# Block 2's context attention: a new first pass, its logits and norms moved among the feed-forward's products, and the weights' loads placed in the first pass

## The chip, the cores and the metric

The kernel runs on one core of one Trainium2 chip. A time is the device time of one execution in microseconds (us). The profile names the engines PE (TensorE matmuls; PEld is its weight loads), DVE (VectorE), ACT (ScalarE), POOL (GpSimd) and SP (SyncE, which here only issues DMAs). Its times are counted from the start of the span of one profiled execution.

## The reference

Four transformer blocks of the same width run one after the other over x, 4 sequences of 1024 tokens with 288 columns; the context has 64 tokens of 288 columns per sequence. Block 2 (`_L2_xattn_ref`) is the one that matters: self attention, then attention to the context, then a gated feed-forward, each added to x. Its second half is:

```python
n2 = _ln(h, ln2_g, ln2_b)
h = h + _quant_attention(n2, ctx, Wq2, Wk2, Wv2, Wo2, bo2)
n3 = _ln(h, ln3_g, ln3_b)
a, gate = jnp.split(n3 @ Wff1 + bff1, 2, axis=-1)      # 288 -> 2 x 1152
h = h + a * jax.nn.gelu(gate, approximate=False) @ Wff2 + bff2

# in _quant_attention, 16 heads of 18 columns:
q, k, v = _fake_quant(q, 8), _fake_quant(k, 8), _fake_quant(v, 8)
probs = softmax(q k^T / sqrt(18))
probs = _fake_quant(probs, 8, always_zero=True)        # delta = max over ALL probs / 255
out = (probs v) @ Wo + bo
```

The step of the probabilities' quantization is the maximum over every token, head and sequence. So all logits must be seen once (largest probability and sum of each row) before the first probability can be rounded, and the context attention takes two passes.

## The kernel before, in words

x stays on the chip as 32 tiles of 128 tokens (`self.x`). `fq_tail` does the second half of block 2. It receives the queries' raw values in DRAM (`rawq`) and the keys and values in three block-diagonal forms (`kbd4`, `kbd`, `vbd`), also in DRAM.

First pass, one tile of 128 tokens at a time: the queries are rounded to levels on DVE (L818, L819, L3426), transposed on PE (L3432), copied by ACT to `qT` (L3436) and stored to `qb` in DRAM (L3437). Four matmuls give the logits of 16 heads by 64 keys with the tokens on the partitions (L3442); ACT takes the exponential (L3449), DVE the largest of each head (L3455), POOL adds halves and quarters (L3457, L3459), and DVE sums what is left (L3460). After the 32nd tile `prob_shift` works out the step and a shift for each row of logits (L2546 to L2560, L836 to L844).

Then the loads for the feed-forward are issued: `w1` (3456 KB, L2582), `w2` (1296 KB, L114), the bias (L3476) and three broadcasts by POOL (L108).

Second pass, in groups of four tiles (512 tokens). `probs(t0)` loads `qT` back (L3486), adds the shift (L2567 on POOL, L2573 on PE, L2574 on DVE), takes the logits with the keys on the partitions (L3500, L3504), rounds them (L3506), multiplies by the values (L3512, L3519) and by `wo` (L278), and adds to x (L3525). `forward(t0)` takes the norm's statistics (L1437 to L1468), norms each tile (ACT L1485, POOL L1488 and L1489, with the bias added to x by POOL at L1877), transposes it (`width_T`: L2591, L2596, copy L2603), does the first product in blocks of four columns of 128 (`product4`: L2611, L2615), the gated Gelu (L3552, L3556), and the second product (L3564) that is added to x (L3572). A float32 matmul of the source is two instructions in the trace. The two are interleaved by `weave`: `probs` of one group with `forward` of the group before it and eight pieces of `spare`, which prepares block 3's weights (L1629 to L1700).

The order in which the source calls is not the order on the engines: a scheduler places the instructions by priority, engine by engine, and allocates the tiles from pools with a fixed number of buffers; each engine then executes in its order. Every DMA of these stages but the POOL broadcasts is issued by SP, in one queue. In the second pass two PSUM pools are in use, `pf` with five buffers for the first product and `pb` (`ps1`) with three for everything else. The normed tile `h` has two buffers.

Of the kernel before, what the change touches and what calls it, by code (L numbers as in the profile page):

```python
# [28 lines left out]
F32 = mybir.dt.float32  # L29
BF16 = mybir.dt.bfloat16  # L30
I32 = mybir.dt.int32
AF = mybir.ActivationFunctionType
ALU = mybir.AluOpType
AX = mybir.AxisListType
PSUM = bass.MemoryType.PSUM

P = 128
B, S, C, H, D, T, FF = 4, 1024, 288, 16, 18, 64, 1152
NTB = S // P
# [1140 lines left out]
class Fast(Net):  # L1180
# [2204 lines left out]
    def fq_tail(self, w, kq, keep, rawq, mx, nmn, beside):  # L3385
# [5 lines left out]
        with ExitStack() as es:  # L3391
# [3 lines left out]
            nc.sync.dma_start(wo, w["Wo2p"].rearrange("(g p) o -> p g o", p=P))  # L3395
            kt = {k: gp.tile(keep[k][1], BF16, name=k) for k in ("kbd", "vbd")}
            qb = [dr.tile([P, NG, S], BF16, name=f"qb{b}") for b in range(B)]
            with (
                self.psum8("f2"),
                tc.tile_pool(name="f2q", bufs=1) as qp,  # L3400
                self.work("f2k0", 3),
            ):
                kt["kbd4"] = qp.tile(keep["kbd4"][1], BF16, name="kbd4")
                for k, (d, _) in keep.items():
                    nc.sync.dma_start(kt[k], d)
                top = qp.tile([P, NT, H], F32, name="top")
                sums = qp.tile([P, NT, H], F32, name="sums")
                qn = qp.tile([P, NT, C], F32, name="qn")
                for b in range(B):
                    nc.sync.dma_start(qn[:, b * NTB : (b + 1) * NTB, :], rawq[b])  # L3410
                pads = [qp.tile([P, H, HP], BF16, name=f"pads{n}") for n in range(3)]
                for pd in pads:
                    nc.gpsimd.memset(pd, 0.0)
                q = self.global_params(gp, mx, nmn, "qq")
                self.watch_range(-0.5, 255.5, q["zp"], "qzext")
                step = gp.tile([P, 1], F32, name="step")
                nc.vector.tensor_scalar(
                    step, q["d"], kq["d"][:, 0:1], SCALE, ALU.mult, ALU.mult
                )
                rstep = self.scale_register("cstep", step)  # L3420

                for t in range(NT):
                    b, j = divmod(t, NTB)
                    pd = pads[t % 3]
                    self.fq_levels(qn[:, t, :], q, 0)
                    nc.vector.tensor_scalar(  # L3426
                        pd[:, :, :D], self.heads(qn[:, t, :]), q["top"], None, ALU.min
                    )
                    ps = self.ps1(BF16)
                    pf = pd.rearrange("p h d -> p (h d)")  # L3430
                    for g in range(NG):
                        nc.tensor.transpose(  # L3432
                            ps[:, g * P : (g + 1) * P], pf[:, g * P : (g + 1) * P], self.idb
                        )
                    qT = self.wk.tile([P, NG, P], BF16, tag="qT1", name="qT1")
                    nc.scalar.copy(qT, ps[:, : NG * P].rearrange("p (g t) -> p g t", t=P))  # L3436
                    nc.sync.dma_start(qb[b][:, :, j * P : (j + 1) * P], qT)  # L3437
                    e = self.wk.tile([P, H, T], F32, tag="e1", name="e1")
                    for m in range(2):
                        ps = self.ps1()  # L3440
                        for g in (2 * m, 2 * m + 1):
                            nc.tensor.matmul(  # L3442
                                ps[:, (g % 2) * 256 : (g % 2 + 1) * 256],
                                lhsT=qT[:, g, :],
                                rhs=kt["kbd4"][:, b, g, :],
                                start=True,
                                stop=True,
                            )
                        nc.scalar.activation(  # L3449
                            e[:, 8 * m : 8 * m + 8, :],  # L3450
                            ps.rearrange("p (h k) -> p h k", k=T),
                            AF.Exp,
                            scale=rstep,
                        )
                    nc.vector.tensor_reduce(top[:, t, :], e, AX.X, ALU.max)  # L3455
                    e2 = self.wk.tile([P, H, T // 2], F32, tag="e2", name="e2")
                    nc.gpsimd.tensor_tensor(e2, e[:, :, : T // 2], e[:, :, T // 2 :], ALU.add)  # L3457
                    e4 = self.wk.tile([P, H, T // 4], F32, tag="e4", name="e4")
                    nc.gpsimd.tensor_tensor(e4, e2[:, :, : T // 4], e2[:, :, T // 4 :], ALU.add)  # L3459
                    nc.vector.tensor_reduce(sums[:, t, :], e4, AX.X, ALU.add)  # L3460
                pd, parts = self.prob_shift(gp, qp, top, sums, step)
            pv = gp.tile([P, 1], F32, name="pv")
            nc.vector.tensor_tensor(pv, pd, kq["d"][:, 1:2], ALU.mult)
# [2 lines left out]
            spads = [gp.tile([P, H, HP], BF16, name=f"spad{n}") for n in range(2)]  # L3466
            for sp in spads:
                nc.gpsimd.memset(sp, 0.0)
            wp = pool("f3w", 1)
            g3 = self.load_bc(wp, w["ln3_g"], C, "g3")  # L3470
            b3 = self.load_bc(wp, w["ln3_b"], C, "b3")
            nf = FF // P
            w1 = self.load_w3(wp, w["Wff13"], 2 * FF, "w1")
            w2 = self.load_w(wp, w["Wff2"], C, "w2", p=P)
            bf1 = wp.tile([P, 2 * nf], F32, name="bf1")
            nc.sync.dma_start(bf1, w["bff1"])  # L3476
            bf2 = self.load_bc(wp, w["bff2"], C, "bf2")
            self.pf = pool("f3p", 5, space=PSUM)
            self.pb = pool("f3q", 3, space=PSUM)
            es.enter_context(self.work("f2k"))  # L3480

            def probs(t0):

                b, j0 = divmod(t0, NTB)
                qT = self.wk.tile([P, NG, 512], BF16, tag="qT2", name="qT2")
# [2 lines left out]
                for j in range(4):  # L3488
                    t = t0 + j
                    self.add_shift(qT[:, :, j * P : (j + 1) * P], spads[t % 2], parts, t)  # L3490
                    yield
                oT = self.wk.tile([P, NG, 512], F32, tag="oTc", name="oTc", bufs=1)
                ebs = []

                for g in range(NG):
                    e = self.wk.tile([P, 2, 512], F32, tag="ec", name="ec")
                    for pr in range(2):
# [7 lines left out]
                    eb = self.wk.tile([P, 2, 512], BF16, tag="ebc", name="ebc", bufs=4)  # L3505
                    nc.vector.tensor_scalar(eb, e, MAGIC, MAGIC, ALU.add, ALU.subtract)  # L3506
                    ebs.append(eb)
                yield
                for g in range(NG):
                    ps = self.ps1()  # L3510
                    for pr in range(2):
# [13 lines left out]
                    nc.vector.tensor_tensor(xt, xt, ps[:, :C], ALU.add)  # L3525
                    yield

            def forward(t0):
                stats = self.norm_stats_of(t0, 4, 1e-5)
                yield  # L3530
                hT = self.wk.tile([P, 3, 512], F32, tag="hT", name="hT", bufs=1)
                hs = {}
                for j in range(5):
                    if j < 4:
                        hs[j] = self.tmp(C, "h")
                        self.norm_apply(hs[j], t0 + j, stats, g3, b3, t0)
                        self.add_bias(t0 + j, bf2)
                        yield
                    if j:
                        self.width_T(hT[:, :, (j - 1) * P : j * P], hs[j - 1])  # L3540
                        yield
                us = []
                for f0 in range(0, nf, 2):
                    fs = range(f0, min(f0 + 2, nf))
                    cols = [c for f in fs for c in (nf + f, f)]
                    pss = [self.pf.tile([P, 512], F32, tag="F", name="psf") for _ in cols]
                    self.product4(
                        pss, lambda i: w1[:, :, cols[i] * P : (cols[i] + 1) * P], lambda i: hT
                    )
                    for n, f in enumerate(fs):  # L3550
                        gl = self.wk.tile([P, 512], F32, tag="gl", name="gl")
                        nc.scalar.activation(  # L3552
                            gl, pss[2 * n], AF.Gelu, bias=bf1[:, nf + f : nf + f + 1]
                        )
                        u = self.wk.tile([P, 512], F32, tag="u", name="u", bufs=nf + 2)
                        nc.vector.scalar_tensor_tensor(  # L3556
                            u, pss[2 * n + 1], bf1[:, f : f + 1], gl, ALU.add, ALU.mult
                        )
                        us.append(u)
                    yield  # L3560
                for j in range(4):
                    ps = self.ps1()
                    for f in range(nf):
# [4 lines left out]
                            start=(f == 0),  # L3568
                            stop=(f == nf - 1),
                        )  # L3570
                    xt = self.x[:, t0 + j, :]
                    nc.vector.tensor_tensor(xt, xt, ps[:, :C], ALU.add)  # L3572
                    yield

            spare = beside(pool("f2p", 1))

            def some(n):
                while n and next(spare, spare) is not spare:
                    n -= 1
                    yield  # L3580

            before = None
            for t0 in range(0, NT, 4):
                gens = [probs(t0)] + ([forward(before), some(8)] if before is not None else [])
                self.weave(gens, 3, 1)
                before = t0
            for _ in spare:
                pass
            self.weave([forward(before)], 1, 1)

    def scale_register(self, name, t):

# [174 lines left out]
```

## Time and profile before

| | us |
|---|---|
| median of 3 runs (4857.51 to 4862.07) | 4860.33 |
| the profiled execution: its time / its span | 4857.3 / 4855.6 |
| first pass, from the first rounding to the last sum | 2877.7 to 2987.5 |
| first `psf` matmul of the first group | 3072.9 |
| last matmul of the second product | 3670.3 |

PE is busy for 87% of the span, DVE for 63%, ACT for 61%, POOL for 25%. The granted TensorE clock is 0.863 in the mean. The stage that the change touches lies between 2850 and 3670 us. A table of windows has for each stretch the busy time of each engine with the number of instructions in brackets, the granted clock of PE, the busy share of the DMA engines and what they moved. Busy time of PE is a matter of the clock: the same work takes twice as long at 0.50.

### The profile page before, as it was taken

To read this page: it belongs to the slowest core of one execution; us is meant where nothing else is said; L and a number is where in the kernel's file an instruction comes from. 1 tells how busy PE (TensorE), PEld (TensorE's weight loads), DVE (VectorE), ACT (ScalarE), POOL (GpSimd) and SP (SyncE) were. 2 spreads that over 40 slices of the span, in tenths; PEclk is the share of its full clock that TensorE was granted. 3 is DMA by queue.
4 is the path that set the end of the run, shared out by engine and by line. 5 is a ranking of instruction groups with operands and counts; after the bars stand their busy time and mean duration, and the time that the engine had idled before them with its cause. 6 is when DMAs were issued, how large, how long until landed. Compare 5 with 4: busy or idle time off the path is not lost. (4 is left out here: it accounts for less than half of the span.)

```text
span 4855.6 us, 63549 instructions
## 1 busy us (share of the span) xinstructions
PE 4230.4 (87%) x23227; PEld 1727.3 (36%) x23227; DVE 3038.4 (63%) x6791; ACT 2980.8 (61%) x4227; POOL 1213.9 (25%) x1800
## 2 busy tenths in 40 slices
PE   4999998889988989999788863899998999998886
PEld 2223223445565421110133331445543233223443
DVE  8355445876543579999789977423244345446885
ACT  2776775666652279999799943212114776775664
POOL 2001001433212566420034343111111001002453
PEclk9999999899999965555699975899998999998898
DMA  3000002110001221000001132001000001001000
GB/s 86 4 5 22 9 11 71 44 34 8 13 13 45 109 74 33 26 10 0 20 26 28 28 100 78 20 6 34 1 3 17 2 4 30 7 12 38 15 17 18
DMA packets 137699, 135.97 MB, mean 28 GB/s; under 512 B 69276, under 2 KB 114972, under 8 KB 135712
## 3 DMA queue, kind: packets, MB, share of 16 engines
q1 hardware_dynamic: 136176, 128.13, 8.8%
q0 software_dynamic: 1200, 3.69, 0.4%
q8 instruction: 184, 3.01, 0.3%
q14 instruction: 139, 1.14, 0.1%
HBM read 79.92 MB, written 43.47 MB: 25 GB/s over the span
## 5 line engine op out<-in xcount | busy, mean ns | idle before, releaser
L2148 ACT ACTIVATE e<-ps 128x1024 f32<-128x1024 f32 x1024 | 992.6, 1021 | 410.7 <-PE ps L2138 403.1
L2138 PE MATMUL ps<-qT,kT 32*128 32x512 f32 x4096 | 624.9, 647 | 1.8 <-DVE sext L2060 1.8
L3175 DVE TENSOR_REDUCE top<-e 128x2 f32<-128x2048 f32 x256 | 563.5, 2277 | 14.4 <-ACT e L3168 14.3
L2094 PE MATMUL ps<-e,v 128*32 128x512 f32 x4096 | 553.9, 612 | 9.1 <-DVE oT L2105 9.1
L3603 PE MATMUL ps<-qk 32*128 32x512 bf16 x1024 | 499.6, 604 | 40.7 <-ACT e L3168 38.8
L3168 ACT ACTIVATE e<-ps 128x1024 f32<-128x1024 f32 x512 | 520.1, 1152 | 6.9 <-PE ps L3603 3.7
L3652 ACT ACTIVATE e<-ps 128x1024 f32<-128x1024 f32 x512 | 477.8, 1078 | 33.8 <-PE ps L3643 18.6
L1873 POOL TENSOR_TENSOR x<-x,y 128x288 f32<-128x288 f32 x192 | 152.2, 804 | 832.3 <-DVE y L1872 486.3
L3658 DVE TENSOR_SCALAR eb<-e 128x2048 bf16<-128x2048 f32 x256 | 324.0, 1271 | 48.2 <-ACT e L3652 47.2
L2611 PE MATMUL psf<-hT,w 128*128 128x512 f32 x576 | 257.9, 600 | 0.6 <-ACT hT L2603 0.6
L2138 PEld LDWEIGHTS ps<-qT,kT 32*128 32x128 f32 x4096 | 185.3, 185 | 202.0 <-issue 129.5
L3643 PE MATMUL ps<-qk,kz 64*128 64x512 bf16 x1024 | 215.9, 419 | 33.2 <-ACT e L3652 28.6
L2094 PEld LDWEIGHTS ps<-e,v 128*32 128x32 f32 x4096 | 81.2, 108 | 402.7 <-issue 344.2
L3603 PEld LDWEIGHTS <-qk 32*128 32x128 bf16 x1024 | 52.9, 99 | 465.0 <-issue 464.0
L3552 ACT ACTIVATE gl<-psf,bf 128x512 f32<-128x512 f32 x72 | 46.0, 684 | 268.5 <-PE psf L2615 264.1
L1488 POOL TENSOR_TENSOR h<-h,g 128x288 f32<-128x288 f32 x112 | 91.2, 816 | 442.9 <-ACT h L1485 433.5
L1990 POOL TENSOR_TENSOR v<-y,wv1b 128x288 f32<-128x288 f32 x64 | 51.5, 809 | 562.0 <-DVE y L1987 562.0
L3556 DVE SCALAR_TENSOR_TENSOR u<-psf,bf,gl 128x512 f32<-128x512 f32 x72 | 51.2, 747 | 217.9 <-ACT gl L3552 217.9
L2105 DVE COPY oT<-ps 128x512 f32<-128x512 f32 x64 | 44.2, 690 | 212.1 <-PE ps L2094 212.1
L278 PEld LDWEIGHTS <-qT 98*128 98x128 bf16 (+2 forms) x1344 | 129.6, 103 | 124.1 <-ACT qT L1390 37.4
L3168 ACT ACTIVATION_READ_ACCUMULATOR e<-ps 128x1 f32 x512 | 172.5, 337 | 0.0
L2611 PEld LDWEIGHTS psf<-hT,w 128*128 128x128 f32 x576 | 109.5, 192 | 132.8 <-issue 123.9
(530 smaller groups left out, 7827.1 us busy)
## 6 DMA issues: line engine op xcount, KB each, us to landing
raw<-y SPq DMA_DIRECT2D x32, 432.0 KB
in<-raw SPq DMA_DIRECT2D x30, 432.0 KB
kz<-qk SPq DMA_DIRECT2D x128, 64.0 KB
wn<-in_L_wfc SPq DMA_DIRECT2D x12, 432.0 KB
x<-in_x SPq DMA_DIRECT2D x4, 1152.0 KB
vvo<-vt SPq DMA_DIRECT2D x16, 288.0 KB
vo<-vvo SPq DMA_DIRECT2D x4, 1152.0 KB
rawq<-y SPq DMA_DIRECT2D x32, 144.0 KB
```

The source lines that it names most:

```text
L278: self.nc.tensor.matmul(out, lhsT=lhs[:, k, :], rhs=rhs[:, k, c0:c1], start=(k == 0), stop=(k == kc - 1))
L1873: nc.gpsimd.tensor_tensor(self.x[:, t, :], self.x[:, t, :], y, ALU.add)
L2094: nc.tensor.matmul(acc[i * HP : (i + 1) * HP, :], lhsT=st["v"][:, kt, h * (D + 1) : h * (D + 1) + HP], rhs=es_[i // 2][:, i % 2, :], start ...
L2138: nc.tensor.matmul(pss[i // 2][:, i % 2, :], lhsT=self.row_tile(kT, i)[:, kt * P : (kt + 1) * P], rhs=self.row_tile(qT, i)[:, qh * 512 : ( ...
L2148: nc.scalar.activation(e, ps, AF.Exp, scale=SCALE)
L2611: nc.tensor.matmul(o, lhsT=lhs(i)[:, c, :], rhs=rhs(i)[:, c, :], start=(c == 0), stop=False)
L3168: nc.scalar.activation(e[:, j, :].rearrange("p (a n) -> p a n", a=2), sc, AF.Exp, scale=rstep, accum_out=sums[:, t, h0 + j : h0 + j + 1],)
L3175: nc.vector.tensor_reduce(top[:, t, h0 : h0 + 2], e, AX.X, ALU.max)
L3603: self.last = self.nc.tensor.matmul(ps[:, c, :], lhsT=self.row_tile(qT, i)[:, g, qt * P : (qt + 1) * P], rhs=self.row_tile(kT, i)[:, g, c ...
L3643: nc.tensor.matmul(pss[i][:, n, :], lhsT=kz[rows, i, kt * P : (kt + 1) * P], rhs=qT[rows, g, qh * 512 : (qh + 1) * 512], start=True, stop= ...
L3652: nc.scalar.activation(e[:, 2 * n : 2 * n + 2, :], ps, AF.Exp, scale=step)
L3658: nc.vector.tensor_scalar(eb, e, MAGIC, MAGIC, ALU.add, ALU.subtract)
```

## The change

The loads of the feed-forward's weights move from behind the first pass to the end of its first group of four tiles; the pool that holds them is opened ahead of the pass.

The first pass works on groups of four tiles. `largest` rounds, transposes and stores as before, and DVE takes the largest logit of each head straight from PSUM (one 128x1024 reduction for each tile); the exponential is taken once at the end, of the maxima alone. `total` computes the logits of the group a second time with the keys on the partitions (8 matmuls of 64 rows, 512 columns), takes the exponential with four ACT instructions of 128x1024, sums over the keys with 8 float32 matmuls against a matrix of ones (`pick`, 32 columns each), and turns the sums back with 4 small float32 matmuls (`back`). POOL has no adds left there. The PSUM pools there become three of two banks and two of one bank, where there were eight of one bank.

The second pass is cut into `logits`, `attended`, `norms`, `first` and `second`, and ordered by hand: the logits of group n+1 go among the second product of group n-1, and the loads and shifts of group n+2 among the first product of group n; the norms of a group are issued ahead; and between the second product of one group and the first product of the next stands the rest of the attention of the group after it with the four `width_T`. The `wo` matmuls then stand all ahead of the first product, where 24 of their 32 instructions stood within it.

```diff
+            wp = pool("f3w", 1)
             with (
-                self.psum8("f2"),
+                self.psum_attn("f2"),
...
-                for t in range(NT):
+                def largest(t, qT):
...
-                    e = self.wk.tile([P, H, T], F32, tag="e1", name="e1")
-                    for m in range(2):
-                        ps = self.ps1()
-                        for g in (2 * m, 2 * m + 1):
...
-                        nc.scalar.activation(
-                            e[:, 8 * m : 8 * m + 8, :],
-                            ps.rearrange("p (h k) -> p h k", k=T),
-                            AF.Exp,
-                            scale=rstep,
...
+                    ps = self.ps2()
+                    for g in range(NG):
+                        nc.tensor.matmul(
+                            ps[:, g // 2, g % 2 * 256 : (g % 2 + 1) * 256],
...
+                    nc.vector.tensor_reduce(
+                        top[:, t, :], ps.rearrange("p a (h k) -> p (a h) k", k=T), AX.X, ALU.max
+                    )
+
+                def total(n, qT):
+
+                    es_ = []
+                    for g in range(NG):
+                        ps = self.ps2()
+                        for pr in range(2):
+                            rows = slice(pr * 64, (pr + 1) * 64)
                             nc.tensor.matmul(
+                                ps[:, pr, :], lhsT=kt["kbd"][rows, n // 2, g, :],
+                                rhs=qT[rows, g, :], start=True, stop=True,
...
+                        e = self.wk.tile([P, 2, 512], F32, tag="e1", name="e1", bufs=6)
+                        nc.scalar.activation(e, ps, AF.Exp, scale=rstep)
+                        es_.append(e)
+                        yield
+                    acc = self.ps1()
+                    for pr in range(2):
+                        for g in range(NG):
+                            nc.tensor.matmul(
+                                acc[g * HP : (g + 1) * HP, :], lhsT=pick[:, pr, :],
+                                rhs=es_[g][:, pr, :], start=(pr == 0), stop=(pr == 1),
+                            )
+                    sT = self.wk.tile([P, 512], F32, tag="sT", name="sT")
+                    nc.scalar.copy(sT, acc)
+                    yield
+                    ps = self.ps1()
+                    for j in range(4):
+                        nc.tensor.matmul(
+                            ps[:, j * H : (j + 1) * H], lhsT=sT[:, j * P : (j + 1) * P],
+                            rhs=back, start=True, stop=True,
                         )
-                    nc.vector.tensor_reduce(top[:, t, :], e, AX.X, ALU.max)
-                    e2 = self.wk.tile([P, H, T // 2], F32, tag="e2", name="e2")
-                    nc.gpsimd.tensor_tensor(e2, e[:, :, : T // 2], e[:, :, T // 2 :], ALU.add)
-                    e4 = self.wk.tile([P, H, T // 4], F32, tag="e4", name="e4")
-                    nc.gpsimd.tensor_tensor(e4, e2[:, :, : T // 4], e2[:, :, T // 4 :], ALU.add)
-                    nc.vector.tensor_reduce(sums[:, t, :], e4, AX.X, ALU.add)
...
+                running = []
+                for n in range(NT // 4):
+                    qT = self.wk.tile([P, NG, 512], BF16, tag="qT1", name="qT1")
+                    for j in range(4):
+                        largest(4 * n + j, qT[:, :, j * P : (j + 1) * P])
+                        running = [t for t in running if next(t, running) is not running]
+                    running.append(total(n, qT))
+                    if n == 0:
+                        g3 = self.load_bc(wp, w["ln3_g"], C, "g3")
...
+                        w1 = self.load_w3(wp, w["Wff13"], 2 * FF, "w1")
+                        w2 = self.load_w(wp, w["Wff2"], C, "w2", p=P)
...
+                nc.scalar.activation(top, top, AF.Exp, scale=rstep)
                 pd, parts = self.prob_shift(gp, qp, top, sums, step)
...
-            wp = pool("f3w", 1)
-            g3 = self.load_bc(wp, w["ln3_g"], C, "g3")
...
-            w1 = self.load_w3(wp, w["Wff13"], 2 * FF, "w1")
-            w2 = self.load_w(wp, w["Wff2"], C, "w2", p=P)
...
-            before = None
             for t0 in range(0, NT, 4):
-                gens = [probs(t0)] + ([forward(before), some(8)] if before is not None else [])
-                self.weave(gens, 3, 1)
-                before = t0
-            for _ in spare:
-                pass
-            self.weave([forward(before)], 1, 1)
+                hs = []
+                normed = norms(t0, hs)
+                for i, _ in enumerate(second(t0 - 4, us) if t0 else none):
+                    next(scored if i % 2 else spare, None)
+                    if i in (0, 2, 4):
+                        next(normed)
+                while len(hs) < 2:
+                    next(normed)
+                hT = self.wk.tile([P, 3, 512], F32, tag="hT", name="hT", bufs=1)
+                after = attended(t0 + 4, nxt) if t0 + 4 < NT else none
+                for j in range(4):
+                    next(after, None)
+                    self.width_T(hT[:, :, j * P : (j + 1) * P], hs[j])
+                    next(normed, None)
+                drain(after)
+                if t0 + 4 >= NT:
+                    drain(spare)
+                nxt, us = [], []
+                scored = logits(t0 + 8, nxt) if t0 + 8 < NT else none
+                for _ in first(hT, us):
+                    next(scored, None)
+                    next(spare, None)
+            drain(second(NT - 4, us))
```

## The prediction

> **What bounds the kernel now.** I read the chain of waits first, then windows of the stage, then the timeline of PE in it. The chain (start, us, what) shows where the stage from 2850 to 3670 us loses time without work:
>
> ```profile
> 3008.54 10.37 SPq L3476
> 3019.73 7.43 DMA qT<-qb
> 3035.23 9.39 PE ps L278 x32
> 3115.91 17.67 PE ps L3564 x72
> ```
>
> SP stands 10.37 us in one DMA issue because the 4752 KB of `w1` and `w2` ahead of it fill its queue, and the 512 KB of `qT` behind them then take 7.43 us: one queue, served in order, at about 0.35 MB/us. From there on the chain is PE. The windows (us, then busy time of PE, PEld, DVE, ACT and POOL with counts, PE's granted clock, DMA share, GB/s):
>
> ```profile
> 2875.00:2880.00 5.00, 0.57 (x4) 0.35 (x4) 3.97 (x24) 0.38 (x1) 0.37 (x1) 0.50 1.02 394
> 2878.00:2989.00 111.00, 49.77 (x256) 27.17 (x256) 94.84 (x172) 52.95 (x97) 64.20 (x64) 0.50 0.28 73
> 3015.00:3020.00 5.00, 0.00 (x0) 0.00 (x0) 0.00 (x0) 0.00 (x0) 0.00 (x0) 0.50 1.03 386
> 3140.00:3145.00 5.00, 4.76 (x28) 1.94 (x26) 4.05 (x8) 3.05 (x7) 0.39 (x1) 0.54 0.41 119
> 3160.00:3200.00 40.00, 40.00 (x133) 20.14 (x130) 12.20 (x32) 6.89 (x11) 4.54 (x6) 1.00 0.00 0
> ```
>
> The first pass has PE at half clock and DVE nearly full. In the second pass PE has no gap within the products, at clock 1.00, and drops to half clock between the second product of one group and the first of the next. How that happens is seen on PE's timeline:
>
> ```profile
> 3450.21 0.37 PE L3500 MATMUL ps<-qT,kbd 64*128 64x512 bf16 x1 [0.27 <-ACT hT L2603]
> 3452.65 2.54 PE L3500 MATMUL ps<-qT,kbd 64*128 64x512 bf16 x5 [2.06 <-ACT ec L3504]
> ...
> 3461.65 3.71 PE L278 MATMUL ps<-wo,oTc 128*128 128x288 f32 x8
> ...
> 3604.43 0.42 PE L2596 MATMUL ps<-idf,h 128*32 128x128 f32 x8
> 3604.79 0.44 PE L2591 MATMUL ps<-idf,h 128*128 128x128 f32 x2
> 3605.15 0.43 PE L2596 MATMUL ps<-idf,h 128*32 128x128 f32 x8
> 3608.34 0.69 PE L2591 MATMUL ps<-idf,h 128*128 128x128 f32 x2 [2.76 <-POOL h L1489]
> 3608.96 0.66 PE L2596 MATMUL ps<-idf,h 128*32 128x128 f32 x8
> 3610.59 0.69 PE L2591 MATMUL ps<-idf,h 128*128 128x128 f32 x2 [0.97 <-POOL h L1489]
> 3611.21 0.65 PE L2596 MATMUL ps<-idf,h 128*32 128x128 f32 x8
> 3612.46 10.02 PE L2611 MATMUL psf<-hT,w 128*128 128x512 f32 x16 [0.60 <-ACT hT L2603]
> ```
>
> The last rows are the last group, where no attention is left: with two normed tiles ready and two buffers, the third `width_T` waits 2.76 us for POOL, the fourth 0.97, and the 16 matmuls after it take 10.02 us in place of 6.87 (the chain's row for the others). The change brings every group into this pattern.
>
> **The change part by part.** The sum is made against the profiled execution (4857.3 us; 1.7 around its span). The median shown is 3.0 above it.
>
> 1. *Weights' loads.* The wait that goes: 16.1 us of DVE for `qT` after 3011. What they collide with instead: the built order of the changed kernel has SP issue `w1` and `w2` not after the first group but among the last four stores of `rawq`, ahead of `kbd4` and of all four loads of `qn` (1152 KB each). That is the queue of the first fence at an earlier time. `w1` would go out at 2863.2 (behind the store of 2862.8) and take 3456 KB / 0.35 = 10 us to about 2874. The store of 2868.4 lands behind it, near 2876, in place of 2871.8, when the row "ACT L3314 ... 1.11 <-DMA rawq<-y" has ACT go on (one buffer `y2`). ACT's next copy, DVE's minimum and maximum, and the store after them wait for that; this store then lands behind `w2`, near 2879.6, and the last copy is at 2879.8 in place of 2875.0: the step of the queries is 4.8 us late. `kbd4` and the first `qn` go out after it on SP, 2880.5, and need 1.5 + (1024 + 1152 KB) / 0.35, to about 2888.7. The first rounding on DVE was at 2877.7, so the pass starts 11.0 us later. Bounds: 5 (a store slips between), 14. POOL's three broadcasts and the bias are small and move along.
>
> 2. *First pass.* It was 109.8 us, 13.7 for four tiles. DVE after: 4 x (3 x 0.36 for the rounding, as L818 takes it when POOL is silent, + 1.21 as L3455) + 0.2 for the copied sums = 9.4 us. ACT: 4 x 0.59 (L3436) + 4 x 1.02 (L2148, the same shape) + 0.6 = 7.0. POOL: 64 us of adds go, and with them DVE's stretched roundings of up to 1.35. PE at half clock: what it has now, 49.77 / 8 = 6.2; 8 logits, two at a time on 64 rows, 1.7; 8 sums = 16 instructions, as L2094 runs them four abreast (8 in 1.06 at full clock) 2.1, at half clock 4.2; 4 small ones with 8 weight loads, 2.0; sum 14.1 at half clock, 7.5 at full. So PE becomes the bound at half clock, DVE at full. The stage's clock decides, and no row shows this mixture: bounds 9.4 and 14.1 + 2 of waits in order (each `K` waits for ACT's copy of the transpose before it, the sums for the last exponential). The sums are full-array float32 like the `wo` product, whose 32 instructions at 3035 pulled the clock from 0.50 to 1.00 in 3 us; I take 12. Behind the last tile stand one chain of 4 exponentials, sums, copy, turn: 8 us where 3 stood. 8 x 12 + 8 = 104: -5.8.
>
> 3. *Up to the first product.* From the last sum (2987.5) to the first `psf` (3072.9) 85.4 us. The 16.1 of part 1 go; the 24 `wo` instructions of the next group that were within the first product come ahead, 24 x 0.2425 = 5.8. The rest (norms of group 0 at POOL's 2.34 a tile, cold PE) stays: -10.3. The extra exponential of the maxima (0.6 on ACT) lies beside the last sums.
>
> 4. *Six groups, 78.5 us each* (3543.8 - 3072.7 = 471.1). After, for one group, by these rows: second product 4 x (18 x 0.2425) = 17.5; four pairs of logits among it, 0.4 each, and after each the next tile of `ps1` (three buffers: two hold logits, the third waits for DVE's add to x, 0.75 us after the product's end) costs 0.45: 20.8. Then value product, `width_T` 0.73, twice; the third `width_T` needs `h`: ACT's copy (behind the last two exponentials, 2 x 0.62), ACT 0.63, POOL 3 x 0.79: PE is idle 2.6 us and then 1.1, as in the last fence, and `wo` starts at 29.7. The 32 `wo` take 7.8, plus 2.2 if cold (8 took 3.71 at 3461 for 1.96). First product 36.0 (4.5 blocks of 16 x 0.43 + 1.1), 16 shift transposes 1.3, 0.3 for the five `psf` buffers. Sum 77.3. That ACT has the next group's two norms queued ahead of the Gelu costs nothing: they end near 5 us into the first product, and the first Gelu is due at 8; with the statistics 3 us later it would cost. `spare` moves from the gap to the products; DVE has 12 of 40 us busy there.
>
> Here the Trainium skill speaks for more: "TensorE: Matmul & The Clock Gate", What's actually happening, ties the drop to half clock to a whole idle window of about 3.4 us, and no gap here is that long. Then `wo` would be warm and `width_T` short: 74.6. But the row at 3452 has the drop with one idle stretch of 2.06, in every group, and at 3608 with 2.76. I take the row: 6 x (77.3 - 78.5) = -7.2; by the page -23.4.
>
> 5. *Seventh group*: 68.7 before, with 6.6 of `wo` in its first product; those now stand in part 4's stretch: -6.6. The last two products are as before.
>
> Sum: +11.0 - 5.8 - 10.3 - 7.2 - 6.6 = -18.9, or 4838.4; with the 3.0 to the median, 4841.
>
> **The rivals.**
> *Clock stays up* (0.22). PE's fuller queue holds 1.00 through the first pass (10 us a group, -16) or through the stretch of part 4 (-16), or `w1` delays less. For: fewer waits on PE; against: transposes and value products at over 90% busy stayed at 0.54 in 3140:3145. 4809 to 4825.
> *PE bounds the new pass* (slower, 0.17). Float32 sums on a half-clock PE: 14.1 us of work and 2.4 of waits in order, 16.5 a group, 8 x 16.5 + 9 = 141, +37: 4878, or 4870 with a smaller start delay. It decides from 15.6 us a group on. For: 0.50 all through this pass now. Against: the mixture is dense.
> *Given back* (0.16). At 15 us a group the pass takes 128, and what the weights' wait gave is eaten by it and by the 11 us: within 10 us of no change, near 4862.
> *The loads don't hide*: as part 1 has it, at its upper bound; it shifts any case by 3.
>
> **How the numbers follow.** The case worked out has 0.45 (4828 to 4853 by its bounds), clock up 0.22, given back 0.16, slower 0.17. 0.2% is 9.7 us, about what can be told from no change. Of the first case a tenth lies above 4850.6: faster 0.65, same 0.17, slower 0.18. Range 4808 to 4873.
>
> **What would show it.** SP's issue of `w1` ahead of `qn`, and the first rounding near 2889; no wait of `qT` for a DMA after the pass; the pass's clock, and its length near 104; the third `width_T` waiting about 2.6 us for POOL in every group, and `wo` slow for its first 8; groups of 77 us. A first pass over 125 us, or groups over 79, would prove it wrong.

## The result: 26 us faster, 0.9946 of the time before

The changed kernel takes 4834.75 us (median of 5 runs, 4829.8 to 4836.18) against 4861.16 us of the kernel before (5 runs): a ratio of 0.9946, 95% interval 0.9933 to 0.996. The prediction had 4841, 19 below the time before it was given; 26 were measured.

Two profiled executions drift against each other by some microseconds in stages that the change does not touch. So all places below are counted from one event that every kernel has just ahead of the stage, ACT's copy `hT` (L3303) after its long wait for PE (19.3 us in both), "the mark": 2858.56 us in the kernel before, 2861.50 after.

| us after the mark | before | after | difference grows by |
|---|---|---|---|
| first rounding | 19.1 | 32.0 | +12.9 |
| last sum of the first pass | 128.9 | 121.0 | -20.9 |
| first `psf` matmul, group 1 | 214.3 | 193.0 | -13.4 |
| the same, group 7 | 685.1 | 662.7 | -1.0 |
| the same, group 8 | 753.9 | 728.1 | -3.5 |

The sum is -25.9, the medians differ by 26.4. In the profiled spans (4855.6 and 4834.2) it is 21.4 only: the mark itself stands 2.9 us later after, and the rest comes behind the stage.

**The profile after.** First SP's issues and DVE's first rounding (start us, us, engine, line, operation, out<-in, count; in brackets the idle time before it and who ended it):

```profile
2865.74 0.32 SPq L3316 DMA_DIRECT2D rawq<-y  x1
2866.10 0.43 SPq L2582 DMA_DIRECT2D w<-in_L_Wff  x1
2871.31 0.32 SPq L3316 DMA_DIRECT2D rawq<-y  x1
2871.68 0.43 SPq L114 DMA_DIRECT2D w<-in_L_Wff  x1
2879.56 0.32 SPq L3316 DMA_DIRECT2D rawq<-y  x1
...
2883.55 0.32 SPq L3316 DMA_DIRECT2D rawq<-y  x1
2885.53 0.32 SPq L3406 DMA_DIRECT2D kbd<-dkbd  x1
2885.90 2.27 SPq L3411 DMA_DIRECT2D qn<-rawq  x4
...
2893.52 0.65 DVE L818 TENSOR_SCALAR qn<-qn,qqrd 128x288 f32<-128x288 f32 x2 [6.70 <-DMA qn<-rawq]
...
3007.45 1.52 DVE L2574 TENSOR_TENSOR qT<-qT,ps 128x512 bf16<-128x512 bf16 x4 [0.20 <-DMA qT<-qb]
```

`w1` and `w2` go out among the last stores of `rawq`, `kbd4` and all of `qn` behind the last store, and DVE starts after waiting for `qn`. The last row is what replaces the wait that DVE had for `qT` before the change, 0.20 us in place of 16.12:

```profile
3027.14 1.52 DVE L2574 TENSOR_TENSOR qT<-qT,ps 128x512 bf16<-128x512 bf16 x4 [16.12 <-DMA qT<-qb]
```

The windows (us, busy time of PE, PEld, DVE, ACT, POOL with counts, PE's granted clock, DMA share, GB/s) show the new pass:

```profile
2905.00:2915.00 10.00, 8.43 (x45) 3.58 (x44) 8.88 (x19) 5.83 (x8) 0.00 (x0) 0.68 0.21 53
2915.00:2925.00 10.00, 9.17 (x67) 4.20 (x64) 7.27 (x15) 6.60 (x9) 0.00 (x0) 1.00 0.21 54
2945.00:2955.00 10.00, 9.13 (x68) 4.27 (x70) 8.52 (x19) 6.59 (x9) 0.00 (x0) 1.00 0.24 60
```

PE is busy for nine tenths of the time and has full clock from 2915 on; before it had 0.50 in the whole pass. Then PE's timeline between two products of the second pass, and at one place of the fourth group:

```profile
3115.05 0.41 PE L3562 MATMUL ps<-ebc,vbd 128*64 128x512 bf16 x2 [0.65 <-DVE x L3625]
...
3119.67 0.69 PE L2591 MATMUL ps<-idf,h 128*128 128x128 f32 x2 [2.09 <-POOL h L1489]
3120.29 0.66 PE L2596 MATMUL ps<-idf,h 128*32 128x128 f32 x8
3120.87 0.64 PE L3562 MATMUL ps<-ebc,vbd 128*64 128x512 bf16 x2
3121.92 0.69 PE L2591 MATMUL ps<-idf,h 128*128 128x128 f32 x2 [0.41 <-POOL h L1489]
3122.54 0.66 PE L2596 MATMUL ps<-idf,h 128*32 128x128 f32 x8
3123.13 9.61 PE L278 MATMUL ps<-wo,oTc 128*128 128x288 f32 x32
...
3333.56 0.75 PE L3615 MATMUL ps<-w,u 128*128 128x288 f32 x2 [2.60 <-DVE u L3604]
```

The third `width_T` waits for POOL's `h`, PE falls to half clock (0.69 us in place of 0.44 for a transpose like the first one's, L2591), and the 32 `wo` instructions take 9.6 us, in later groups up to 10.5. The last row is a new wait: DVE makes a `u`, the second product's input, late. From one group's first `psf` to the next take 78.1, 78.1, 78.0, 82.0, 76.2 and 77.4 us.

### The profile page after: what moved, and what is told of

Read it like the earlier page. It is cut to its first block, busy times and chain, and to the rows that moved or that the text cites. A ratio compares the mean times of both kernels' runs of the same rounds, so it can differ in the third digit from the quotient of the medians.

```text
span 4834.2 us, 63890 instructions
## 1 busy us (share of the span) xinstructions
PE 4243.8 (88%) x23483; PEld 1732.9 (36%) x23483; DVE 3012.5 (62%) x6767; ACT 2984.3 (62%) x4204; POOL 1149.3 (24%) x1742
## 5 line engine op out<-in xcount | busy, mean ns | idle before, releaser
L3168 ACT ACTIVATE e<-ps 128x1024 f32<-128x1024 f32 x512 | 520.1, 1152 | 6.9 <-PE ps L3677 3.7
L1485 ACT ACTIVATE h<-x,nmr,rstd 128x288 f32<-128x288 f32 x112 | 67.2, 633 | 152.7 <-DVE nmr L1468 100.1
```

What stands on the lines that cost most here:

```text
L3168: nc.scalar.activation(e[:, j, :].rearrange("p (a n) -> p a n", a=2), sc, AF.Exp, scale=rstep, accum_out=sums[:, t, h0 + j : h0 + j + 1],)
```

## The experiments

Times are medians of the runs; each set has its own runs of the kernel before, so the ratio (and its interval) is what compares. "Saved at group 8" is by how much the first `psf` matmul of group 8 stands closer to the mark than in the kernel before, in the profiled run.

| kernel | us | ratio to before | saved at group 8 |
|---|---|---|---|
| changed | 4834.75 | 0.9946 (0.9933, 0.996) | 25.9 |
| before, loads early | 4848.78 | 0.9982 (0.9973, 0.9991) | 10.4 |
| before, new pass | 4832.97 | 0.9947 (0.9934, 0.9959) | 22.8 |
| changed, loads late | 4834.66 | 0.9947 (0.9934, 0.996) | 26.0 |
| changed, low pool | 4813.15 | 0.9899 (0.9884, 0.9914) | 41.8 |
| changed, low pool and loads held | 4810.35 | 0.9893 (0.9878, 0.9908) | 45.3 |
| changed, bfloat16 sums | 4835.18 | 0.9944 (0.993, 0.9958) | 26.3 |
| changed, four `h` | 4790.03 | 0.9858 (0.9844, 0.9872) | 63.3 |
| changed, logits behind | 4833.92 | 0.9944 (0.9931, 0.9958) | 24.4 |
| changed, four `h`, logits behind | 4800.77 | 0.9874 (0.9858, 0.9891) | 50.3 |
| changed, pieces in the first product | 4831.45 | 0.9935 (0.9922, 0.9949) | 31.6 |
| low pool, loads held, four `h` | 4776.27 | 0.9825 (0.9811, 0.9838) | 83.3 |
| the same, pieces in the first product | 4771.83 | 0.9816 (0.9803, 0.9829) | 83.8 |

**The kernel before with the loads early.**

```diff
+            wp = pool("f3w", 1)
             with (
                 self.psum8("f2"),
...
                     nc.vector.tensor_reduce(sums[:, t, :], e4, AX.X, ALU.add)
+                    if t == 3:
+                        g3 = self.load_bc(wp, w["ln3_g"], C, "g3")
...
```

> The kernel before with one part of the change: the weights' pool opened ahead of the first pass and its loads placed after four tiles. By the prediction's terms the pass starts 11 to 13 us later and the 16 us of waiting for qT go: 3 to 5 us below the kernel before, near 4857. Rival: the time at the turn is set by the rounding of the probabilities' shift and not by qT; then it is 5 to 13 us slower, 4866 to 4874.

It is 7 us faster by the medians, where the prediction's terms gave 3 to 5. In its profile:

```profile
2889.29 0.65 DVE L818 TENSOR_SCALAR qn<-qn,qqrd 128x288 f32<-128x288 f32 x2 [6.48 <-DMA qn<-rawq]
3015.25 1.52 DVE L2574 TENSOR_TENSOR qT<-qT,ps 128x512 bf16<-128x512 bf16 x4 [0.21 <-DMA qT<-qb]
```

The mark is at 2857.91, so the pass starts at 31.4, 12.3 late, as in the changed kernel; the wait for `qT` is gone. The step of the loads has both terms, whatever the pass. A third thing is in no term: the old pass takes 101.8 us here in place of 109.8 (DVE waits 9.3 us in it for POOL and ACT, before it was 16.0). That is most of the 10.4 us saved at group 8; why the waits are shorter stays open.

**The kernel before with the new first pass.** The loops `largest` and `total` in place of the old one, loads behind.

> The kernel before with another part of the change: the new first pass (sums on PE, exponentials over four tiles), the weights loaded after it as before. If the pass is worth what the two traces say, 109.8 to 88.9 us, it is 21 us faster than before, near 4840, with the pass at full clock and the wait for qT still there. Rival: the pass was short in the changed kernel only because its input came late and in one piece; then it takes over 100 us here and the kernel is within 10 us of before, 4851 to 4861.

The pass takes 88.7 us (it starts 19.4 and ends 108.1 after the mark): 21 less than before, and the kernel is as fast as the changed one. But

```profile
3007.02 1.52 DVE L2574 TENSOR_TENSOR qT<-qT,ps 128x512 bf16<-128x512 bf16 x4 [19.75 <-DMA qT<-qb]
```

the wait for `qT` has grown from 16.12 to 19.75. Pass alone 22.8 and loads alone 10.4 make 33.2 us, and the changed kernel with both and a new second pass has 25.9. Where the two meet: the loads cost 12.6 us at the start, and from the last sum to the first addition to `qT` they bring only 11.2 (36.2 in this kernel, 25.0 in the changed one). The rest is work on DVE, pieces of block 3's weights. This kernel does 9.0 us of them within the pass, the changed one all of them behind it: 8.6 us before the shift of the probabilities is ready (`parts`, L2558; 3.4 in this kernel) and 3.3 after. The load of `qT` itself waits for that shift, as a row of SP's waits in the changed kernel says (us in all, how often, the longest):

```profile
SPq L3534 <- DVE parts L2558: 10.5, 1, 10.5
```

It goes out at 3003.63, and the addition starts at 3007.45. So pieces ahead of the shift delay the load, and those behind it fill the time in which it is under way. With the new pass, the early loads brought nothing on balance (first addition 144.2 us after the mark in this kernel, 145.9 in the changed one; first `psf` 191.4 and 193.0). No run has both with the second pass as it was, or with those pieces elsewhere.

**What makes the start late: queue or memory.** In the changed kernel `kbd4` waits not for SP's queue alone: ahead of it SP runs five instructions that wait for DVE, PE, POOL and several DMAs. The longest of these waits ends when the last store of `rawq` lands:

```profile
SPq L3406 <- DMA rawq<-y: 1.3, 1, 1.3
```

In the kernel before nothing of the kind stands there; `kbd4` goes out behind the first of these stores. The reading that the runs test is memory: the weights' pool, opened ahead, pushes the pass's own pool up, to where the stage before still works. Three kernels were made to divide this. The first holds `w1` back until the pass runs, and `w2` in the same way two groups later:

```diff
+                    if n == 1:
+                        w1 = wp.tile([P, 3, 2 * FF], F32, name="w1")
+                        nc.vector.tensor_copy(w1[:, 0, :1], top[:, 4 * n, :1])
+                        nc.sync.dma_start(w1, w["Wff13"].rearrange("(c p) o -> p c o", p=P))
...
```

> The changed kernel with w1 and w2 issued in the second and fourth group of the new first pass (each tile first written from a maximum of that pass, so that SP can't issue it sooner). If the two loads among the stores of rawq made the step of the queries late, the first rounding moves from 2893.5 back to about 2881, and the transfers hide in the pass: 12 us below the changed kernel, near 4823. Rival: the stores of qb behind the loads then hold up the pass or the first qT, and nothing is gained: 4832 to 4838.

The first rounding comes at 24.6 in place of 32.0, not at 19: without the weights in the queue 7.4 of the 12.9 are gone. `kbd4` and `qn` still go out behind the last store. Nothing was gained in the end, for another reason than the rival's: the pass takes 95 us in place of 89, also in its later groups, where no load runs. The instructions stand in another order there, with all eight transposes of two tiles together, and PE waits 1.11 us for ACT's copy behind them, once a group; its clock was 0.83 in one window of 10 us (2945 to 2955) and 1.00 in most others. So as a test of the loads alone this run is unclean.

The second and third put `kbd4` and the first quarter of `qn` into a pool below the weights'; the last line of the diff, with its like for `w2`, is in the third alone:

```diff
+            lo = pool("f2l", 1)
             wp = pool("f3w", 1)
...
-                qn = qp.tile([P, NT, C], F32, name="qn")
+                qs = [k.tile([P, n * NTB, C], F32, name="qn") for k, n in ((lo, 1), (qp, B - 1))]
...
+                        nc.gpsimd.tensor_copy(w1[:, 0, :1], qs[1][:, NT - NTB - 1, :1])
```

Low pool alone:

> The changed kernel with kbd4 and the first quarter of qn in the pool below the weights' alone; w1 and w2 are not held and stand again on SP among the last stores of rawq and ahead of the other three quarters. It divides the late start. If the memory makes it: the first rounding stays near its place in the run with both (19 us after the last transposed tile's copy of the stage before, where the changed kernel has 32), 4810 to 4816. If the weights in the queue make it, as the prediction had it: 26 to 30 us after, 4824 to 4834.

Low pool and loads held:

> The changed kernel with kbd4 and the first quarter of qn in a pool below that of the weights, so that they don't lie in memory that the stage before still uses; w1 and w2 are held until the last quarter of qn has landed. Theory A (the pass starts 13 us late since kbd4 and qn wait for that memory, and for the weights in the queue): its first rounding comes 12 us earlier, the rest of the pass is fed in time, and the kernel is 9 to 12 us below the changed one, near 4824. Theory B (the three quarters that still wait for memory come too late, and the pass stops after eight tiles): 0 to 4 us below, 4831 to 4835.

```profile
2866.57 0.43 SPq L3413 DMA_DIRECT2D qn<-rawq  x1
...
2875.43 1.37 SPq L3413 DMA_DIRECT2D qn<-rawq  x3
...
2875.75 0.43 DVE L818 TENSOR_SCALAR qn<-qn,qqrd 128x288 f32<-128x288 f32 x1
```

This is the third kernel. The first quarter of `qn` is on its way before the last two stores, as before the change, and the first rounding is back at 19.3 (the mark is at 2856.47). In both `kbd4` is back behind the first of the stores, so it was memory that it waited for. Low pool alone has the first rounding at 19.0, but then DVE stands 3.5 us for POOL's zeroed `pads`, and the other three quarters go out at 2886.3, behind the weights. At the last sum, where the changed kernel stands at 121.0, low pool alone has 112.1 and the third kernel 108.4. But low pool alone did not hold the queue: `w1` and `w2` go out behind the third and the fourth of the last stores there, in place of the first and the second,

```profile
2873.29 0.43 SPq L2582 DMA_DIRECT2D w<-in_L_Wff  x1
2876.08 0.32 SPq L3316 DMA_DIRECT2D rawq<-y  x1
2876.44 0.43 SPq L114 DMA_DIRECT2D w<-in_L_Wff  x1
2886.32 1.27 SPq L3413 DMA_DIRECT2D qn<-rawq  x3
```

so that no store waits for them (ACT waits 1.05 us for the third store's buffer, 5.47 in the changed kernel). The 8.9 us are therefore what the low pool makes through memory and queue together; 3.7 more come when the loads are held too. How much each makes alone was not separated. The time of the low pool came out as its first case had it; the third kernel saves 12 us more than expected. At group 8 it is 19.4 us ahead of the changed one: 11.9 up to the first `psf`, 5.4 in the six groups (the fourth has 77.3 us there and no late `u`), 2.2 in the seventh. The rest of its 24 is within the runs' intervals.

**What set PE's clock in the pass.** The prediction saw the float32 sums as what might raise it.

```diff
-                pick = qp.tile([P, 2, HP], F32, name="pick")
+                pick = qp.tile([P, 2, HP], BF16, name="pick")
...
-                        e = self.wk.tile([P, 2, 512], F32, tag="e1", name="e1", bufs=6)
+                        e = self.wk.tile([P, 2, 512], BF16, tag="e1", name="e1", bufs=6)
```

> The changed kernel with the exponentials of the first pass and the 0-1 matrix that sums them in bfloat16, so that no wide float32 product is left in the pass but the 8 small ones of each four tiles; the sums lose digits by it. Theory A (PE reached full clock because its queue had hardly a gap): the clock still reaches 1.00 within the first group or two and the pass stays at 86 to 92 us, or it falls back once PE has gaps. Theory B (the float32 sums raise the clock, as the prediction argued): 0.50 to 0.6 through the pass and 96 to 110 us, so 8 to 20 us slower than the changed kernel.

The pass takes 87.8 us at a mean granted clock of 0.81 (the changed kernel's: 89.0 at 0.92), so theory B falls. One group of this kernel, and its window:

```profile
2927.10 0.62 PE L3445 MATMUL ps<-idb,pads 128*128 128x128 bf16 x8
2928.83 1.04 PE L3452 MATMUL ps<-kbd,qT 128*128 128x256 bf16 x4 [1.11 <-ACT qT L3448]
2929.80 0.61 PE L3470 MATMUL ps<-qT,kbd 64*128 64x512 bf16 x2
2930.34 1.04 PE L3452 MATMUL ps<-kbd,qT 128*128 128x256 bf16 x4
...
2932.79 0.61 PE L3452 MATMUL ps<-kbd,qT 128*128 128x256 bf16 x4
...
2945.00:2955.00 10.00, 8.38 (x56) 4.33 (x56) 8.20 (x18) 6.53 (x9) 0.00 (x0) 0.83 0.25 52
```

All eight transposes of two tiles stand together here, as in the run with the loads late, and PE runs dry for 1.1 us behind ACT once a group. For the next 3 us the four matmuls of L3452 take 1.04 us in place of 0.61; then the clock is back, without a float32 product in between. In the changed kernel the same four matmuls take 1.04 us at 2906.4 and 0.61 at 2908.5, 4 us before its first sum (2912.8). That rise did not last: behind 1.27 us of idle time the clock fell once more, and it stays up from 2914.7 on, within the first sums. Here it rises at 2914.9, with sums in bfloat16. So float32 is not what raises it; work on PE with hardly a break fits all these rows.

What the clock is worth in this pass stays open. The steady groups take 10.1 to 10.2 us here at 0.83 and 9.6 in the changed kernel at 1.00, but this kernel has less work on PE and another order. Which chain sets the length was not separated.

**The norms: four buffers for `h`.**

```diff
-                    h = self.tmp(C, "h")
+                    h = self.wk.tile([P, C], F32, tag="h", name="h", bufs=4)
...
-                    if i in (0, 2, 4):
+                    if i in (0, 2, 3, 4, 5):
                         next(normed)
-                while len(hs) < 2:
+                while len(hs) < 4:
```

> The changed kernel with four buffers for the normed tile h in place of two, so that all four norms of a group run within the second product. Theory A (the wait of the third and fourth width_T for POOL, 2.09 and 1.1 us, also drops PE's clock): both waits go, the products of wo fall from 10.4 us to about 7.8 in each group, 6 us a group and as much before the last one: about 42 us below the changed kernel, near 4793. Theory B (the clock falls in this stretch whatever the wait, because value products and transposes are short): only the waits go, 3.2 us a group: about 23 below, near 4812, wo still at 10 us. Theory C (POOL still late, or ACT's four queued norms hold up the first Gelu): within 5 us of the changed kernel, 4835.

Theory A, to 3 us. The same stretch as in the profile after, and its window:

```profile
3114.90 0.44 PE L2591 MATMUL ps<-idf,h 128*128 128x128 f32 x2 [0.26 <-ACT hT L2603]
...
3116.68 8.03 PE L278 MATMUL ps<-wo,oTc 128*128 128x288 f32 x32
...
3112.00:3125.00 13.00, 12.63 (x82) 8.27 (x82) 6.87 (x16) 2.51 (x6) 0.00 (x0) 1.00 0.13 41
```

The wait for POOL is gone, and with it the drop of the clock: `wo` takes 8.03 us. The fifth and sixth group take 71.4 us each where 76.2 and 77.4 stood: waits for POOL of 2.5 and 3.2 us cost 4.8 and 6.0. At group 8 it is 37.4 us ahead of the changed kernel; by the ratios it is 43, by the medians 45.

**The logits' place.** Behind the second product, as they stood before the change:

```diff
-                    next(scored if i % 2 else spare, None)
+                    if i % 2 == 0:
+                        next(spare, None)
...
                 while len(hs) < 2:
                     next(normed)
+                drain(scored)
```

> The changed kernel with the logits of the next group put back behind the second product (the shift stays in the first product, the norms stay ahead, two buffers for h). Theory A (the 3 us that the logits and their waits add to the second product are less than what they cost in the gap, where PE waits for eight exponentials): 2 to 5 us a group slower, 6 groups: 4847 to 4865. Theory B (the third width_T waits for POOL anyway, and the logits fill that wait): the same within 4 us, 4831 to 4839.

Theory B: the time is that of the changed kernel. The eight logits take 3.1 us at full clock there:

```profile
3110.70 0.39 PE L3545 MATMUL ps<-qT,kbd 64*128 64x512 bf16 x2
3111.38 2.72 PE L3545 MATMUL ps<-qT,kbd 64*128 64x512 bf16 x6 [0.29 <-DVE x L3625]
3114.22 0.41 PE L3562 MATMUL ps<-ebc,vbd 128*64 128x512 bf16 x2
...
3119.00 0.44 PE L2591 MATMUL ps<-idf,h 128*128 128x128 f32 x2 [2.10 <-POOL h L1489]
```

and the wait for POOL behind them is the same. So it was asked again where no wait covers them:

> The changed kernel with four buffers for h and the logits of the next group put back behind the second product. Without the wait for POOL nothing is left to hide the logits behind. If they are worth something within the second product, it shows here: PE then waits for the exponentials in the gap (8 of 0.62 us on ACT), 2 to 5 us a group, so 12 to 30 us above the run with four buffers and the logits within, 4802 to 4820. If their place doesn't matter: 4786 to 4794.

By the medians it is 11 us slower than four `h` with the logits within, by the ratios 8, and the intervals overlap; at group 8 of the profiled runs it is 13.0 behind. In the last two groups before group 7 the place is worth little: 71.65 us a group against 71.4. In the second, third and fourth group it is not: 77.1, 76.0 and 79.0 us against 72.6, 72.0 and 76.2. PE has as many instructions there and no wait over 0.3 us that the other run lacks, but its granted clock over the group is 0.93 to 0.94 in place of 0.98 to 1.00. Two stretches of the second group show where it falls, two of the fifth where it does not:

```profile
3185.32 2.72 PE L3545 MATMUL ps<-qT,kbd 64*128 64x512 bf16 x6 [0.29 <-DVE x L3625]
...
3185.56:3188.97 3.41, 2.72 (x10) 0.79 (x8) 2.22 (x4) 3.41 (x8) 0.00 (x0) 1.00 0.00 0
3188.97:3199.21 10.24, 10.21 (x55) 5.12 (x54) 3.14 (x5) 2.03 (x5) 0.00 (x0) 0.50 0.17 53
3415.96:3419.37 3.41, 2.62 (x8) 0.67 (x7) 1.92 (x4) 3.41 (x8) 0.00 (x0) 1.00 0.00 0
3419.37:3422.78 3.41, 3.06 (x37) 1.40 (x36) 2.78 (x5) 1.50 (x4) 0.00 (x0) 1.00 0.00 0
```

The logits come at the pace of ACT, which is busy for all of the 3.41 us; PE takes 2.72 us for six that are 0.37 us each, with short gaps between them, and half clock follows for 10.24 us (in the third group as long, in the fourth 6.83). So the place of the logits matters once no other wait covers it, by the clock and not by their own time, and in three of six groups. Why not in the others these rows don't tell: PE was busy for less of the stretch in the fifth group, and its clock stayed up.

**The long fourth group.** The pieces woven into the first products only:

```diff
-                    next(scored if i % 2 else spare, None)
+                    if i % 2:
+                        next(scored, None)
```

> The changed kernel with the pieces of the next block's weights woven into the first products alone and no longer into the second ones. If the fourth group's 82 us (others 76 to 78) come from such pieces ahead of a Gelu's product on DVE, the pieces spread over more groups, no group is over 78.5 and the kernel is 3 to 5 us faster than the changed one, near 4831. If DVE has the same pieces in a row at another place, another group is long, and the time is the same within 2 us.

The groups are 78.5, 76.3, 77.7, 76.1, 77.4 and 78.9 us: the 82 is gone, and 5.7 us are saved at group 8. The medians differ by 3.3 in the same direction, within their intervals.

**Together.** Low pool, held loads and four `h`:

> The kernel of the run before this one with four buffers for h as in the first run (and ten for u in place of eleven, for memory). If the two are independent: 45 us for the norms and 9 to 12 for the start, near 4780. If ten buffers for u hold up the first product, some us are lost again: 4785 to 4795.

4776.27 us, all of what was expected, with groups of 71.4 to 72.7. And with the pieces in the first products alone:

> The run with the low pool, the held weights and four buffers for h, with the pieces of the next block's weights woven into the first products alone. That run had no long group left, so at most 2 us: 4774 to 4778. If pieces are left over at the last group, where they are all run before its last products, up to 10 us slower: 4778 to 4786.

At group 8 it stands 0.5 us better; the medians differ by 4.4, within their intervals. Both beat the changed kernel by about 60 us and the one before by 84 to 88.

## Why the prediction was right, and where only its sum was

The sign and the time held, the terms less well: the first pass gave 15 us more than was predicted, the seven groups together 9 less, and part of the one covered the other. That the sum came within 7 us of the result is in part luck.

1. *Weights' loads.* Sized well: +11.0 predicted, +12.9 measured, and the wait for `qT` went from 16.12 to 0.20. Its path through the stores held: ACT waited 5.47 us for the third store's buffer, and the step of the queries came 5.2 us late where 4.8 were worked out. The last sum of the working is a little off (2880.5 + 1.5 + 6.2 makes 2888.2 and not 2888.7, so 10.5). What it took for a mere place in the queue is more: `kbd4`, with `qn` behind it, follows the last store because it waits for memory that the stage before still uses. With `kbd4` and the first quarter of `qn` in a low pool 8.9 us at the last sum were gone, memory and queue together.
2. *First pass.* The term that was mis-sized most: 12 us a group were taken between 9.4 and 16.1, for -5.8; it took about 9.6 a group in the steady part (`L3481` starts at 2923.31, 2932.92 and 2942.53), -20.9 in all. The rival *Clock stays up* is what happened, in the first of its forms (10 us a group). That "the stage's clock decides" is not shown: with bfloat16 sums the pass is as long at a mean clock of 0.81. The reason given for the middle value was wrong: the clock first rose ahead of the sums, and it rises without float32 ones.
3. *Up to the first product.* -10.3 predicted, -13.4 measured.
4. *Six groups.* -7.2 predicted, -1.0 measured. 77.3 a group was right for five of the six (77.5 in the mean); the fourth has 82.0, since pieces of `spare` on DVE delay a `u`. "DVE has 12 of 40 us busy there" was read from the kernel before, where those pieces stood elsewhere. The pattern itself held: 2.09 of waiting for POOL where 2.6 were worked out, up to 1.1 behind it, `wo` 9.3 to 10.5 where 10.0 was taken.
5. *Seventh group.* -6.6 predicted, -3.5 measured: the 6.6 us of `wo` went, and the first product, with the rest of the pieces ahead, has 1.87 us of waiting for `u`.

The rule that was weighed in part 4, "TensorE: Matmul & The Clock Gate", What's actually happening, ties the half clock to a whole idle window of about 3.4 us. The runs side with the row: after 2.09 us of idle time and less around it the clock dropped (in two of the six gaps at once, in the others only behind the second, shorter wait), and with that wait taken out it stayed at 1.00 through all of the stretch. In the run with bfloat16 sums 1.1 us of idle time was followed by about 3 us at half clock. In the run with four `h` and the logits behind, the clock fell after 3.41 us of which PE was busy for 2.72. The half-clock stretches there last 6.83 and 10.24 us, two and three times 3.41: a window of the rule's length shows, an idle one isn't needed. What share of it decides can't be told from these rows.

The slower rival, PE bounding the new pass at half clock, needed a half clock that lasts; with PE nine tenths busy and no gap over 0.34 us in the steady part, it did not.

## What to carry to other kernels

A pool that is opened earlier can move the ones behind it to memory that is still in use: look at what the first loads wait for, not only at where they stand in the queue. A short wait on PE costs itself and the half clock behind it (here 2.5 and 3.2 us of waits were 4.8 and 6.0), so buffers that let another engine run ahead can be worth more than moving PE's own work: two more tiles of 1152 bytes in each partition, with the norms issued earlier, brought 37 us up to group 8. The place of the logits brought nothing while that wait stood, and 13 us there with the wait gone. And gains that meet at the same wait are to be added on the path and not on paper: up to the first `psf`, 22.9 and 10.8 us made 21.3.

## What the runs showed of the hardware that was not expected

PE's clock fell after idle times of 2.09 us, of 1.1 us in the run with bfloat16 sums, and after 3.41 us with short gaps between matmuls of 64 rows (PE busy for 2.72). It came back after 3.4 to 10.2 us there, with bfloat16 work as with float32.
